# A spectral mixer in two halves: own tiles for x1 in the first images, half 1's inverse transforms and first loads ahead of the output blocks, and norms beside a transform

## The chip, the cores and the metric

The kernel runs on one core of one Trainium2 chip. The metric is the device time of one execution in microseconds, as the median of several runs. One core has five engines that work side by side, each through its own queue of instructions in order: TensorE (PE, with weight loads as PEld), VectorE (DVE), ScalarE (ACT), GpSimd (POOL) and SyncE (SP), which here only issues transfers. Transfers are also issued by ScalarE and GpSimd. A transfer that waits at the head of a queue holds up whatever stands behind it in that queue.

## The reference

The input x is an array of 256 x 256 pixels of 128 channels. Two layers are added to it one after the other. Layer 0 (a group norm and an attention with gate and biases) is not touched by the change. The result of layer 0 is x1, and layer 1 is `x1 + L1(gn(x1))`. It begins with a spectral attention over 256 tokens, images of 128 x 128 pixels, and ends with a mixer of four tokens at a time, to which the change belongs:

```python
attn = instance_norm(attn + tokens, attn_norm_w, attn_norm_b)
attn = attn.reshape(b * (C // TOKEN_CODIM), TOKEN_CODIM, H, W)      # groups of 4
h0 = instance_norm(attn, norm2_w, norm2_b)
h1 = fno_layer(h0, ..., norm=True, act=True)
h2 = fno_layer(h1, ..., norm=True)
out = instance_norm(h2, mon_w, mon_b) + attn
# fno_layer(x):
#   skip = einsum('bihw,oi->bohw', x, sw) + sb
#   xf   = instance_norm(spectral_conv(x))     # rfft2, 32 x 16 modes times weights, irfft2
#   y    = xf + skip;  gelu(y) if act
```

So each of the two spectral convolutions of the mixer takes an image to a few modes, mixes the modes within groups of four, and takes them back to an image. The norms in between need sums over the whole image, and so nothing can go from one stage to the next before all blocks of pixels are done.

## The kernel before, in words

Up to about 1,904 us the kernel computes layer 0, the attention of layer 1 and its modes. The mixer begins there. The 256 token images are taken in two halves, `a` = 0 and 1, of 128 images, one image to a partition. The 128 x 128 pixels of an image are split into 16 blocks of `NB` = 2,048 pixels (half a block is `HB` = 1,024). [...]`blocks`, also called `hb[b]`, holds 128 x 16 x 2,048 numbers. Half 1 waits in DRAM as `yd` in the meantime, and so does the residual of half 0 (x1 plus its scaled y) as `wd`. Half 1's images overwrite the blocks of half 0 as these are finished.

The mixer has these stages, each a Python generator that gives way at its `yield`s:

- `y_blocks(a)`: attn + tokens before its norm, one half block at a time, from x1 (`load_x1`, tag "xt") and inverse-transformed modes `gs`: matmuls L1324 and L1200 into `yps`, VectorE's scaling L1334 and statistics L1336. Half 0 goes to `blocks`, half 1 to DRAM (`yd`, L1338, issued by GpSimd).
- `first_modes(a)`: statistics of y (`bn_aggr`, L1418), two norm chains, the modes `F` of half a (loaded at L1412), then `mix_modes` (L1341): 16 products on VectorE (L1358), each with a matmul (L1367), squares (L1370), energy (L1376), the norm, and `Z` (L1399). Then the inverse transform over rows in four chunks (`synth_modes`), each written to DRAM as `Gd1` by copies L584 and transfers L589.
- `first_images(a)`: 16 blocks of `h1 = gelu(spectral part + skip)`: `gs2` loaded by L1217, matmuls L1211 and L1200 into `ups`, Gelu L1495 by ScalarE, four transposes L1504, copies to `hT`, the forward transform over columns `psA` L1527, its copy `yA` L1529 by ScalarE and the write to `Yd` L1530. For half 0 the residual is prepared beside it: `load_w` loads x1 (L1468, `xw`), `add_w` scales the block (L1475, ScalarE) into the second half of the same `xw` tile, adds (L1478, GpSimd) and writes `wd` (L1479). Its three buffers have the tag "xt". For half 1, `load` also brings y of the block from `yd` (L1461).
- `second_modes(a)`: loads `YT_0` to `YT_3` from `Yd` (L1546), transforms over rows (`f1ps`, L1563), copies to `F` (L1569), mixes as above with the second weights, four chunks to `Gd2`, and the last norm (`kap`, `c0`).
- `output_0` and `Output1`: per block the second inverse transform `h2ps`, ScalarE's scaling L1615, VectorE's add of the residual L1621 and the write L1622, issued by GpSimd. For half 1 the residual comes from `yd` and x1 at the time (L1659, L1663), and one VectorE instruction adds them (L1668). `Output1.ahead` does the first five of these during the second mixing.

The order of the work is written out by hand: inside `tc.manual_schedule` each engine keeps the order in which Python emits the instructions, and SyncE's queue is among them. `weave(main, side)` advances the second generator by the time the first says that it has used. The stages follow each other like this, with the times of the trace of before:

- y of half 0 (1,904 to 2,045 us), then first mixing of half 0 with 24 half blocks of y of half 1 (to 2,194), then the first images of half 0 (to 2,341).
- The last eight half blocks of y of half 1, woven with the forward transform of half 0 (to 2,402). Then both mixings at once, step by step in turn: second of half 0 (`m0`), first of half 1 (`m1`).
- Five output blocks of half 0, two steps after each chunk of `m1` (to about 2,533).
- The pools of this part are closed and `hp1` and `op0` opened, and first images of half 1 run beside the remaining output blocks of half 0 (to 2,705).
- Second mixing of half 1 (to 2,784), then its output (to the end).

The driver for the middle part, lines shortened by what does not matter here:

```python
m0 = second_modes(0, wp, tiles(wp), bq, [(xp, "xt", 3)])
weave((1.5 * t for t in iter(lambda: next(m0), None)), y1)
...
for _ in m0:
    next(m1)
...
for t in m1:
    next(o0)
    next(o0)
```

Of the kernel before, what the change touches and what calls it, by code (L numbers as in the profile page):

```python
# [18 lines left out]
P = 128  # L19
# [493 lines left out]
def layer1(tc, I, C, ident, x1d, upool, U, stats2, mv2, out):  # L513
# [9 lines left out]
    with ExitStack() as ctx:  # L523
# [712 lines left out]
        def run(stage):  # L1236
            for _ in stage:
                pass
# [213 lines left out]
        def first_images(a, wp, yp, psk, pst):  # L1452
# [12 lines left out]
            def load_w(b):  # L1465
                for s in range(2):
                    ys[b, s] = yp.tile([P, 2, HB], FP, tag="xt", name=f"xw_{b}_{s}", bufs=3)
                    nc.sync.dma_start(ys[b, s][:, 0], x1v[:, a, b * NB + s * HB : b * NB + (s + 1) * HB])  # L1468

            def add_w(b):  # L1470

                for s in range(2):
                    px = slice(b * NB + s * HB, b * NB + (s + 1) * HB)
                    t = ys.pop((b, s))
                    nc.scalar.activation(  # L1475
                        t[:, 1], hb[b][:, s * HB : (s + 1) * HB], AF.Identity, scale=h.col[:, 3:4]
                    )
                    nc.gpsimd.tensor_tensor(t[:, 1], t[:, 1], t[:, 0], ALU.add)  # L1478
                    nc.gpsimd.dma_start(wd[:, px], t[:, 1])  # L1479

            load(0)
# [54 lines left out]
        def second_modes(a, wp, mk, psum, gts, gbufs=1):  # L1536
# [6 lines left out]
            def load(c):  # L1543
                YT[c] = wp.tile([P, 2, 2, 512], FP, tag="gt", name=f"YT_{a}_{c}", bufs=gbufs)
                for hc in range(2):
                    nc.sync.dma_start(  # L1546
                        YT[c][:, hc],
                        h.Yd[P * hc : P * hc + P].rearrange("h (r f) t -> h r (f t)", r=2)[
                            :, :, 4 * c * P : 4 * (c + 1) * P
                        ],  # L1550
                    )
# [3 lines left out]
            if gbufs > 1:  # L1555
                load(1)
            for c in range(4):
# [12 lines left out]
                if c + gbufs < 4:  # L1570
                    load(c + gbufs)
                    yield 4.0
# [74 lines left out]
        class Output1:  # L1647
# [23 lines left out]
            def ahead(self):  # L1671
                self.more = self.wp
                for k in range(5):
                    self.load(k)
                    if k > 0:
                        self.add(k - 1)
                    yield 1.0
                self.add(4)
# [28 lines left out]
        with tc.manual_schedule(engines=COMPUTE | {ENG.SP}):  # L1707
# [8 lines left out]
            with yctx:  # L1716
# [7 lines left out]
                with tc.tile_pool(name="mp1", bufs=1) as wp:  # L1724
                    y1 = y_blocks(1, br, U1, 32)
                    next(y1)
                    m0 = second_modes(0, wp, tiles(wp), bq, [(xp, "xt", 3)])
                    weave((1.5 * t for t in iter(lambda: next(m0), None)), y1)
                    run(y1)
                    m1 = first_modes(  # L1730
                        1, wp, Tiles(F=(xp, "yt", 2), f=(xp, "yt", 2), m=(xp, "gs", 3)), br,
                        [(wp, "gt", 1), (xp, "xt", 3)],
                    )
                    for _ in m0:
                        next(m1)
# [3 lines left out]
                    for t in m1:  # L1739
                        next(o0)  # L1740
                        next(o0)
                    pools[3] = False
                    next(o0)
                    next(o0)
            with tc.tile_pool(name="hp1", bufs=2) as wp, tc.tile_pool(name="op0", bufs=4) as op:
                pools[:] = [op, wp, 4, True]
                due, begun = 0.0, False
                for done in first_images(1, wp, op, bq, br):
                    if not done:
                        due += 0.72  # L1750
                        begun = due > 0
# [6 lines left out]
            with tc.tile_pool(name="op1", bufs=2) as op:  # L1758
                o1 = Output1(op)
                with tc.tile_pool(name="mp3", bufs=1) as wp, tc.tile_pool(  # L1760
                    name="mpq3", bufs=8, space=PSUM
                ) as psq:
                    m1 = second_modes(1, wp, tiles(wp), Banks(psq, "q"), [(wp, "gt", 2)], gbufs=2)
                    run(iter(lambda: next(m1), None))
                    weave((0.4 for _ in m1), o1.ahead())
# [167 lines left out]
```

## Time and profile before

| | before |
|---|---|
| time, median of 3 runs | 2,918.85 us (2,915.04 to 2,921.63) |
| span of the profiled execution | 2,925.7 us, granted TensorE clock 0.944 |
| instructions | 70,150 |
| busy, share of the span: PE / PEld / DVE / ACT / POOL | 90% / 66% / 69% / 50% / 56% |
| bytes moved | 430.02 MB, 147 GB/s in the mean |

Shares of the whole span say little here, as two thirds of it belong to layer 0 and the attention. The table of windows, cut at the stages named above, gives the busy time in each:

| stage | from to, us | length | PE | DVE | ACT | POOL | DMA share | GB/s |
|---|---|---|---|---|---|---|---|---|
| y of half 0 | 1904 to 2045 | 141 | 139.2 | 87.3 | 0.0 | 0.0 | 0.87 | 278 |
| first mixing half 0, y of half 1 | 2045 to 2194 | 149 | 131.4 | 87.0 | 9.9 | 18.6 | 0.86 | 289 |
| first images half 0 | 2194 to 2341 | 147 | 130.1 | 82.7 | 73.7 | 105.6 | 0.87 | 290 |
| last y of half 1, transform of half 0 | 2341 to 2402 | 61 | 44.9 | 23.2 | 0.6 | 5.1 | 0.81 | 273 |
| both mixings | 2402 to 2471 | 69 | 54.1 | 43.2 | 9.4 | 6.0 | 0.30 | 90 |
| chunks of half 1, five output blocks | 2471 to 2533 | 62 | 28.2 | 16.7 | 19.4 | 11.5 | 0.78 | 262 |
| first images half 1, outputs half 0 | 2533 to 2705 | 172 | 150.5 | 94.2 | 81.1 | 23.3 | 0.85 | 292 |
| second mixing half 1 | 2705 to 2784 | 79 | 47.8 | 31.1 | 7.9 | 6.7 | 0.55 | 170 |
| output half 1 | 2784 to 2925 | 141 | 77.7 | 70.9 | 44.4 | 17.1 | 0.94 | 351 |

Read a row like this: busy times of engines are microseconds within the stage, so an engine whose number is near the length is full. "DMA share" is the mean busy share of the core's 16 transfer engines.

### The profile page before, as it was taken

The page shows a single profiled execution, that of the slowest core. Times are in us where ns is not written, and L with a number is a line of the kernel's source. Part 1 is how long each engine was busy: PE and PEld are TensorE (multiplying, and loading weights), DVE is VectorE, ACT ScalarE, POOL GpSimd, SP SyncE. Part 2 cuts the span into 40 slices and gives each one's busy share as a digit, 9 for nine tenths or more (in the row PEclk, how much of TensorE's full clock was granted, in tenths as well). Part 3 has the DMA queues.
Part 4 walks back from the last instruction along what each step waited for, and adds up shares of the span by engine and source line. Part 5 has one row for each costly group of instructions (what it writes and reads, how often), then busy time and mean ns, then how long its engine had stood idle before and what let it go on. Part 6 is the DMA issues. An engine that isn't in the chain of part 4 may idle for free. (4 is left out here: it accounts for less than half of the span.)

```text
span 2925.7 us, 70150 instructions
## 1 busy us (share of the span) xinstructions
PE 2638.9 (90%) x28524; PEld 1916.9 (66%) x28524; DVE 2007.8 (69%) x3239; ACT 1460.9 (50%) x2844; POOL 1647.0 (56%) x1282
## 2 busy tenths in 40 slices
PE   6799999999999999999999799999898868588654
PEld 6677777777777777777777567777574455344433
DVE  7787888888888888888788645656655545256345
ACT  0477777777777777777777413200005402244032
POOL 0399999999999999999999501100017701111011
PEclk9999999999999999999999899999999988699765
DMA  9422222222222222222222101388798964797599
GB/s 361 165 68 65 72 68 66 66 66 68 66 66 66 67 70 71 66 66 66 68 66 66 44 2 53 114 268 281 251 331 276 304 237 141 263 328 254 168 351 341
DMA packets 240955, 430.02 MB, mean 147 GB/s; under 512 B 26038, under 2 KB 169865, under 8 KB 232312
## 3 DMA queue, kind: packets, MB, share of 16 engines
q1 hardware_dynamic: 200184, 333.24, 34.3%
q0 software_dynamic: 23552, 83.90, 7.8%
q10 hardware_dynamic: 16896, 8.39, 1.0%
q8 instruction: 226, 3.70, 0.5%
q14 instruction: 97, 0.79, 0.1%
HBM read 290.17 MB, written 135.27 MB: 145 GB/s over the span
## 5 line engine op out<-in xcount | busy, mean ns | idle before, releaser
L299 POOL TENSOR_TENSOR e<-e,b1T 128x1024 f32<-128x1024 f32 x256 | 606.6, 2369 | 165.6 <-PE u L348 90.3
L303 POOL TENSOR_TENSOR es<-e 128x512 f32<-128x512 f32 x512 | 639.3, 1269 | 20.1
L281 ACT ACTIVATE sc<-sc,b2T 128x512 f32<-128x512 f32 x512 | 339.0, 662 | 365.5 <-PE sc L272 357.2
L323 DVE RECIPROCAL av<-av 128x256 f32<-128x256 f32 x256 | 452.3, 1767 | 27.2 <-DVE og L322 1.4
L281 ACT ACTIVATE e<-sc,b2T 128x512 f32<-128x512 f32 x512 | 348.0, 680 | 0.0
L294 DVE TENSOR_TENSOR e<-sc,b1T 128x1024 f32<-128x1024 f32 x256 | 311.0, 1215 | 0.0
L272 PE MATMUL sc<-qkT 32*128 32x256 f32 x4096 | 294.3, 401 | 1.3 <-DVE e L294 1.3
L311 PE MATMUL av<-e,v 128*32 128x256 f32 x4096 | 274.7, 385 | 0.5 <-POOL e L299 0.5
L1324 PE MATMUL yps<-xt,mpT 128*128 128x256 f32 x1024 | 244.5, 393 | 21.9 <-DVE yt L1334 11.1
L272 PEld LDWEIGHTS sc<-qkT 32*128 32x128 f32 x4096 | 185.6, 184 | 112.4 <-issue 97.8
L322 DVE SCALAR_TENSOR_TENSOR og<-gate,av 128x256 f32<-128x256 f32 x256 | 107.7, 421 | 190.5 <-PE av L316 190.5
L1324 PEld LDWEIGHTS yps<-xt,mpT 128*128 128x128 f32 x1024 | 194.1, 194 | 60.2 <-DVE yt L1334 14.2
L1338 POOL DMA_DIRECT2D yd<-yt x32 | 17.4, 545 | 358.0 <-DVE yt L1334 358.0
L327 POOL TENSOR_TENSOR x<-xt,bo 128x256 f32<-128x256 f32 x256 | 187.4, 732 | 0.0
L246 PE MATMUL qk<-xnT,wT_wq 128*128 128x256 f32 x512 | 179.5, 432 | 1.7 <-ACT xnT L238 1.7
L252 PEld LDWEIGHTS gv<-wT_wv,kvT 128*128 128x128 f32 x1024 | 155.0, 192 | 13.4
L316 PE MATMUL av<-es,ones 128*32 128x256 f32 x2048 | 157.5, 379 | 2.5 <-POOL es L303 2.5
L333 PE MATMUL wo<-wT_wo,og 128*128 128x128 f32 x1024 | 156.8, 276 | 2.7 <-DVE og L324 2.7
L1615 ACT ACTIVATE blocks<-h2ps,col 128x512 f32<-128x512 f32 x128 | 89.0, 777 | 140.4 <-PE h2ps L1200 140.4
L311 PEld LDWEIGHTS av<-e,v 128*32 128x32 f32 x4096 | 107.0, 109 | 76.1 <-POOL e L299 1.0
L348 PE MATMUL u<-adft,x 128*128 128x129 f32 x1024 | 156.4, 275 | 0.0
L252 PE MATMUL gv<-wT_wv,kvT 128*128 128x128 f32 x1024 | 156.0, 275 | 0.0
(524 smaller groups left out, 5199.4 us busy)
## 6 DMA issues: line engine op xcount, KB each, us to landing
xt<-x1d SPq DMA_DIRECT2D x128, 512.0 KB
xb<-in_x_dram SPq DMA_DIRECT2D x32, 1024.0 KB
xt<-in_x_dram SPq DMA_DIRECT2D x128, 256.0 KB
kt<-in_L_conv_kv_x_dram SPq DMA_DIRECT2D x128, 256.0 KB
x1d<-x SPq DMA_DIRECT2D x256, 128.0 KB
gs<-Gd SPq DMA_DIRECT2D x384, 64.0 KB
yd<-yt POOLq DMA_DIRECT2D x32, 512.0 KB, 5.2
xw<-x1d SPq DMA_DIRECT2D x32, 512.0 KB
```

Source lines behind the costliest of these rows:

```text
L246: nc.tensor.matmul(ps[:, 0:256], wT["wq"], xnT, start=True, stop=True)
L252: nc.tensor.matmul(ps[:, 256 + c * P : 256 + (c + 1) * P], kvT[:, c * P : (c + 1) * P], wT["wv"], start=True, stop=True,)
L272: nc.tensor.matmul(sc[h // 2][:, h % 2, c * 256 : (c + 1) * 256], qkT[p, 256 + c * P : 256 + (c + 1) * P], qkT[p, 0:256], start=True, stop ...
L281: nc.scalar.activation(r["e"][1][:, :, c, :] if hp else z, z, AF.Exp, bias=b2T[:, c, s : s + 1])
L294: nc.vector.tensor_tensor(r["e"][0].rearrange("p h c q -> p (h c q)"), r.pop("sc").rearrange("p h x -> p (h x)"), b1T[:, 0:2].rearrange("p ...
L299: nc.gpsimd.tensor_tensor(e1, e1, b1T[:, 2:4].rearrange("p h c q -> p (h c q)"), ALU.mult)
L303: nc.gpsimd.tensor_tensor(r["es"][hp], e[:, :, 0, :], e[:, :, 1, :], ALU.add)
L311: nc.tensor.matmul(ps[hd, 0:256], r["v"][:, c, hd], r["e"][h // 2][:, h % 2, c, :], start=(c == 0), stop=(c == 1),)
L316: nc.tensor.matmul(ps[32 * h : 32 * h + 32, 256:512], self.ones, r["es"][h // 2][:, h % 2, :], start=True, stop=True,)
L323: nc.vector.reciprocal(rd, rd)
L327: nc.gpsimd.tensor_tensor(r["x1"], r["x"], bc(self.bo, 1, 2), ALU.add)
L1324: nc.tensor.matmul(rows_of(ps[j]), mpT[:, sc, tt], by_turn(xt[:, sc])[:, j], start=(sc == 0), stop=False,)
```

## The change

The change reorders the mixer from the first images of half 0 on, and gives some tiles buffers of their own. The arithmetic and the bytes moved stay the same. It has five parts:

- A, own tiles for x1 in `first_images`. x1's two halves are loaded to tags that other stages had left unused in this one ("yt", two buffers, and a new "xw" with one), and the scaled block gets a whole-block tile `w0` in the three "xt" buffers. Both of ScalarE's scalings go before both of GpSimd's adds. This is meant to free ScalarE from waiting for a write of `wd`.
- B, the norms beside the transform. `second_modes` is told which buffers its four `YT` tiles take. Half 0 now has four of them, and loads 1 after the first transform and 2 and 3 after the second. The last y blocks end before the third transform, and the norm chains of half 1 (`first_modes(1)`) are emitted between the second and the third transform.
- C, half 1's inverse transforms ahead of the output. `m1` runs to its end before output blocks are begun. y and `gs2` of half 1's first block are loaded into tiles of the mixing's pool (`y2`, `g2`), and so they need not wait for the next pools. Two output blocks instead of five come before the change of pools.
- D, as a consequence, more output blocks (14 rather than 11) are run between the images of half 1: the rate is `due += 0.9` instead of 0.72.
- E, in the second mixing of half 1, `Output1.ahead` issues its first two loads at once and does its five adds only after the 16 products of `mix_modes`. The `YT` loads 2 and 3 follow the first and second transform as before.

```diff
-        def first_images(a, wp, yp, psk, pst):
+        def first_images(a, wp, yp, psk, pst, first=None):
...
             def load_w(b):
                 for s in range(2):
-                    ys[b, s] = yp.tile([P, 2, HB], FP, tag="xt", name=f"xw_{b}_{s}", bufs=3)
-                    nc.sync.dma_start(ys[b, s][:, 0], x1v[:, a, b * NB + s * HB : b * NB + (s + 1) * HB])
+                    t = (yp, "yt", 2) if s == 0 else (wp, "xw", 1)
+                    ys[b, s] = t[0].tile([P, HB], FP, tag=t[1], name=f"xw_{b}_{s}", bufs=t[2])
+                    nc.sync.dma_start(ys[b, s], x1v[:, a, b * NB + s * HB : b * NB + (s + 1) * HB])
 
             def add_w(b):
 
+                t = yp.tile([P, NB], FP, tag="xt", name=f"w0_{b}", bufs=3)
                 for s in range(2):
-                    px = slice(b * NB + s * HB, b * NB + (s + 1) * HB)
-                    t = ys.pop((b, s))
-                    nc.scalar.activation(
-                        t[:, 1], hb[b][:, s * HB : (s + 1) * HB], AF.Identity, scale=h.col[:, 3:4]
-                    )
-                    nc.gpsimd.tensor_tensor(t[:, 1], t[:, 1], t[:, 0], ALU.add)
-                    nc.gpsimd.dma_start(wd[:, px], t[:, 1])
-
-            load(0)
+                    px = slice(s * HB, (s + 1) * HB)
+                    nc.scalar.activation(t[:, px], hb[b][:, px], AF.Identity, scale=h.col[:, 3:4])
+                for s in range(2):
+                    px = slice(s * HB, (s + 1) * HB)
+                    nc.gpsimd.tensor_tensor(t[:, px], t[:, px], ys.pop((b, s)), ALU.add)
+                    nc.gpsimd.dma_start(wd[:, b * NB + s * HB : b * NB + (s + 1) * HB], t[:, px])
+
+            if first is None:
+                load(0)
+            else:
+                ys[0], gss[0] = first
...
-        def second_modes(a, wp, mk, psum, gts, gbufs=1):
+        def second_modes(a, wp, mk, psum, gts, yts):
...
             def load(c):
-                YT[c] = wp.tile([P, 2, 2, 512], FP, tag="gt", name=f"YT_{a}_{c}", bufs=gbufs)
+                yp, tag, bufs = yts[c]
+                YT[c] = yp.tile([P, 2, 2, 512], FP, tag=tag, name=f"YT_{a}_{c}", bufs=bufs)
...
-            if gbufs > 1:
+            if a:
                 load(1)
...
-                if c + gbufs < 4:
-                    load(c + gbufs)
+                for k in ((2,), (3,), (), ())[c] if a else ((1,), (2, 3), (), ())[c]:
+                    load(k)
+                if c < 3:
                     yield 4.0
...
             def ahead(self):
                 self.more = self.wp
+                self.load(0)
+                self.load(1)
+                yield 1.0
                 for k in range(5):
-                    self.load(k)
-                    if k > 0:
-                        self.add(k - 1)
+                    self.add(k)
+                    if k < 3:
+                        self.load(k + 2)
                     yield 1.0
-                self.add(4)
...
-                    m0 = second_modes(0, wp, tiles(wp), bq, [(xp, "xt", 3)])
-                    weave((1.5 * t for t in iter(lambda: next(m0), None)), y1)
+                    m0 = second_modes(
+                        0, wp, tiles(wp), bq, [(xp, "xt", 3)], [(wp, "gt", 1)] * 3 + [(xp, "xt", 3)]
+                    )
+                    weave((2.4 * next(m0) for _ in range(3)), y1)
                     run(y1)
                     m1 = first_modes(
-                        1, wp, Tiles(F=(xp, "yt", 2), f=(xp, "yt", 2), m=(xp, "gs", 3)), br,
-                        [(wp, "gt", 1), (xp, "xt", 3)],
-                    )
+                        1, wp, Tiles(F=(xp, "yt", 2), f=(xp, "yt", 2), m=(xp, "gs", 3)), br, [(xp, "xt", 3)]
+                    )
+                    for _ in range(3):
+                        next(m1)
+                    run(iter(lambda: next(m0), None))
                     for _ in m0:
                         next(m1)
                     pools = [xp, xp, 3, True]
                     o0 = output_0(pools, bq)
                     next(o0)
-                    for t in m1:
+                    y2 = wp.tile([P, NB], FP, tag="gt", name="y2_0", bufs=1)
+                    nc.sync.dma_start(y2, ydv[:, 1, 0:NB])
+                    run(m1)
+                    g2 = wp.tile([P, 4, P], FP, tag="m", name="gs2_1_0", bufs=2)
+                    next(o0)
+                    load_modes(g2, halves[1].Gd1, 0)
+                    pools[3] = False
+                    for _ in range(3):
                         next(o0)
-                        next(o0)
-                    pools[3] = False
-                    next(o0)
-                    next(o0)
-            with tc.tile_pool(name="hp1", bufs=2) as wp, tc.tile_pool(name="op0", bufs=4) as op:
+            with tc.tile_pool(name="op0", bufs=4) as op, tc.tile_pool(name="hp1", bufs=2) as wp:
                 pools[:] = [op, wp, 4, True]
                 due, begun = 0.0, False
-                for done in first_images(1, wp, op, bq, br):
+                for done in first_images(1, wp, op, bq, br, (y2, g2)):
                     if not done:
-                        due += 0.72
+                        due += 0.9
                         begun = due > 0
...
-                    m1 = second_modes(1, wp, tiles(wp), Banks(psq, "q"), [(wp, "gt", 2)], gbufs=2)
+                    m1 = second_modes(1, wp, tiles(wp), Banks(psq, "q"), [(wp, "gt", 2)], [(wp, "gt", 2)] * 4)
                     run(iter(lambda: next(m1), None))
-                    weave((0.4 for _ in m1), o1.ahead())
+                    ahead = o1.ahead()
+                    next(ahead)
+                    for k, _ in enumerate(m1):
+                        if k >= 16:
+                            next(ahead, None)
+                    run(ahead)
```

## The prediction, made before the changed kernel was run

> **What bounds the kernel now.** I read the page first: its row of 40 slices shows that from about slice 27 on (1,904 us) no engine is solid, and the DMA row goes down to 1 and 3. The change touches only what begins at 2,184 us, so I cut that part by stage with the table of windows, and then read waits and timeline where a stage has gaps. The window columns are the busy time of PE, PEld, DVE, ACT and POOL, the granted clock, the DMA share and GB/s.
>
> ```profile
> 2218.00:2270.00 52.00, 47.48 (x728) 24.13 (x720) 30.32 (x49) 27.65 (x42) 38.73 (x31) 1.00 0.89 299
> 2345.00:2362.00 17.00, 9.91 (x45) 7.33 (x44) 4.02 (x9) 0.00 (x0) 1.10 (x2) 0.70 0.91 316
> 2400.00:2440.00 40.00, 30.72 (x75) 14.39 (x76) 28.85 (x65) 3.08 (x6) 0.53 (x1) 0.87 0.07 25
> 2505.00:2520.00 15.00, 6.43 (x64) 3.52 (x56) 2.36 (x2) 3.37 (x6) 1.64 (x3) 0.72 0.68 217
> 2520.00:2533.00 13.00, 0.23 (x16) 0.26 (x32) 2.36 (x2) 2.27 (x3) 1.06 (x2) 0.50 0.59 201
> 2610.00:2660.00 50.00, 43.09 (x722) 25.16 (x720) 25.46 (x37) 21.01 (x37) 6.49 (x11) 0.90 0.96 333
> 2732.00:2760.00 28.00, 20.48 (x50) 8.65 (x50) 17.70 (x31) 2.94 (x5) 0.00 (x0) 0.87 0.32 114
> 2850.00:2900.00 50.00, 31.72 (x352) 20.50 (x352) 27.75 (x23) 14.20 (x21) 6.07 (x12) 0.57 1.03 386
> ```
>
> Where blocks stream (rows 1, 2, 6, 8) the transfers are at 0.9 and more, and there the rest hangs on bytes. Between them lie stretches where the DMA idles: the mode mixing, the change-over before half 1's images, the second mixing. A microsecond saved there is a microsecond of the end, since what follows is bound by bytes that have to move anyway.
>
> In half 0's images (from 2,194 us) the timeline and the waits show one loop:
>
> ```profile
> 2264.97 1.15 ACT L1475 ACTIVATE xw<-blocks,col 128x1024 f32<-128x1024 f32 x1 [2.59 <-DMA wd<-xw]
> 2266.03 0.57 ACT L1529 COPY yA<-psA 128x512 f32<-128x512 f32 x1
> 2266.65 0.42 PEld L1504 LDWEIGHTS htps<-ident,blocks 128*128 128x128 f32 x4 [1.38 <-ACT yA L1529]
> ...
> SPq L1468 <- DMA wd<-xw: 80.5, 25, 9.6
> ```
>
> ScalarE's scaling of the next block waits until an old xw buffer has been written out; the copy yA stands behind it in ScalarE's queue, and TensorE's transposes wait for the PSUM bank that yA frees. The starts of ups in that timeline run from 2,218.60 to 2,323.29 us in 12 blocks, 8.72 us each; a block without a stall takes 8.00 (2,270.11 to 2,278.11).
>
> At the change-over to half 1:
>
> ```profile
> 2521.01 1.28 ACT L1495 ACT_TABLE_LOAD   x1
> 2527.10 0.34 SPq L1461 DMA_DIRECT2D y<-yd  x1
> 2532.77 2.02 PE L1211 MATMUL ups<-y,bl 32*32 32x512 f32 x32 [14.20 <-DMA gs<-Gd]
> 2545.34 3.89 PE L1211 MATMUL ups<-y,bl 32*32 32x512 f32 x32 [0.46 <-ACT blocks L1615]
> ```
>
> The first load of half 1 is issued at 2,527, when the new pools' memory is free, which takes the output writes of all blocks before. In the second mixing VectorE's adds for the output stand between the products that TensorE waits for:
>
> ```profile
> 2736.90 1.28 DVE L1668 SCALAR_TENSOR_TENSOR x<-y,col,x 128x1024 f32<-128x1024 f32 x1
> 2737.03 0.43 PEld L1367 LDWEIGHTS z1acc<-z1m,ident 128*128 128x128 f32 x2 [0.65 <-DVE z1m L1358]
> 2759.72 1.29 DVE L1399 TENSOR_TENSOR z1Z<-z1acc,z1rsb 128x512 f32<-128x512 f32 x2 [1.18 <-ACT z1rsb L1396]
> ```
>
> **What the Trainium skill says.** "Perfetto Trace Analysis", section Optimization Strategy: the same gap again and again on the engine that should be full can mean too few buffers for the next tile, and stages with different limits may gain from interleaving. The trace agrees with both: 25 waits of the queue on wd in half 0, and DMA shares of 0.07 and 0.96 in neighbouring stages. "DMA: Bandwidth & Descriptors", section Issuing engines are not separate DMA queues: the transfers of SP, ScalarE and GpSimd share 16 engines. So moving a load ahead adds no bandwidth where the share is 0.96; it fills only idle stretches. The same page, section Anatomy of one DMA, puts most of a transfer's fixed 2 us into the confirmation of the last byte; here under load it is far more, 4.9 us median from issue to landing for wd and 8.0 for the output.
>
> **The change part by part.**
>
> A, half 0's images. The x1 halves get tiles freed by GpSimd's add, and the scaled block a tile of its own in three buffers, so ScalarE waits for a write three blocks old: no stall. Instructions and bytes stay. New waits: xw half 1 has one buffer, so its load waits for the add (2.36 us), and the next block's four gs loads are queued behind it in SP. Add 2.4 plus load 4.5 to 5 (a load issued at about 2,265.0, its add starts at 2,269.89) is 7.3 us, under 8. But bytes then bind: x1 1.05, wd 1.05, gs 0.26, Yd 0.26 is 2.62 MB a block, 8.1 us at 323 GB/s (the mean of 2,552 to 2,660 us). I take 8.35 for 8.72 to 8.9: 13 blocks give 7 us. At the start gs of block 1 is now behind xw, whose slot waits for a yd write issued at 2,191.3 (landing 5.2): 1 to 2 us lost. Net -6.
>
> B, the last eight y blocks with the transform. With GpSimd no longer late, the last yA needn't wait for a Yd write (it waited 8.6 us, TensorE 2.3), so Yd lands and YT_0 is issued some 4 us sooner after the last psA (2,337.1). YT_2 and YT_3, 2.1 MB or 6.5 us at 323 GB/s, go behind the last x1 load, so the y blocks, short of data (row 2), end about 55 us after that psA, not 64.8 (2,401.9). Behind them, bn_aggr and the two norm chains (2,403.1 to 2,411.9, 8.6 us on VectorE) now run alone while YT_2 and YT_3 land, where before they stood between products. -10 for the end of the y blocks; products of half 0 then start 9.5 us after it rather than at once, while half 1's start 14 after it rather than 16.1. By the lockstep of 1.72 us a pair (VectorE and TensorE rows at 2,421 to 2,433) half 0's Z comes at +45 rather than +41.5.
>
> C, the eight inverse transforms in one go, two output blocks instead of five, then half 1. Eight chunks write 1.05 MB each: at 300 GB/s or by three xt buffers (copy 1.3, issue 1.5, landing 5.2) about 3.3 us a chunk, so the last is written at about +79. y of block 0 is loaded before, its gs lands at +84, and block 0 of the images runs at +84, where it stood at +131 (2,532.8). Then a new wait: y of block 1 needs the new pool, hence the output write of block 1: DVE done +86.5, landing 8 later, so +94; gs of output block 2 is behind it in SP, at +103, and ups of block 1 at +105.5 against +143.4 (2,545.3). That is 38 us sooner with three outputs fewer done.
>
> D, the rest of the images. An image costs y 1.05, gs 0.26, Yd 0.26 = 1.57 MB; an output w 1.05, gs 0.26, out 1.05 = 2.36. Before, 16 images and 10 outputs were 48.8 MB in 159.5 us (2,545.3 to 2,704.8), 306 GB/s. Now 13 outputs: 55.8 MB. At 306 it is 182 us; block by block, 13 x 12.2 us (3.93 MB at 323, TensorE needs 9.4) plus three short ones of 6.5, 6.5 and 5 is 177. I take 180: +20. With C, -17 (38 less 20 is 18, less 1 for pool order: YT_0's first half could be issued at 2,694 and now waits for the whole pool).
>
> E, the second mixing. Five adds of 1.28 leave the products: 6.4 us. They go under ScalarE's squares and TensorE's energy sums (2,752.7 to 2,756.6, room for two), the norm's broadcast (1.2) and the first chunk. Loads of blocks 2 to 4 now follow the adds; landing 3.5 us, just in time. -5, and the output stage (386 GB/s, unchanged) moves up by that.
>
> Sum: -6 - 10 - 17 - 5 = -38. I take 3 off for chained estimates: 2,918.85 - 35 = 2,884 us.
>
> **Rivals.** R1, less comes through (bytes): C's gap lasts until +112 and D runs at 295 GB/s (189 us), so that C and D give 2 instead of 17; A and B half, 8; E 5. That is -15, 2,904 us. For: every later stage is at 0.9. Against: 0.96 was held at 2,610 to 2,660. R2, a new wait takes over: the single xw buffer with a landing of 8 us makes a loop of 10.4 us, 15 x 1.7 = 25 us more in A, and D runs at 285 GB/s (196 us, 36 more, C and D together -2 + 1 = -1); with B -10 and E -5 it is +9, 2,928, slower. For: output writes do take 8 us. Against: xw loads landed in 5 with more bytes queued. R3, streaming improves: A at 8.0 (-11), D at 345 GB/s (162 us, 18 better), B and E as above: 2,862. For: 386 GB/s at the end, with large rows. Against: Yd and gs go in short rows. R4, gains and losses cancel, within 6 us.
>
> **How the numbers follow.** The forecast 0.60, R1 0.20, R3 0.09, R2 0.08, R4 0.03. The range reaches from near R3 to past R1: 2,858 to 2,913; outside are R2, R4 and the far end of R3, some 0.17. Faster by over 0.2% (5.8 us): 0.60 + 0.20 + 0.09 = 0.89; same 0.03; slower 0.08.
>
> **What would show it.** In the after profile: ups of half 0 every 8.1 to 8.5 us and no wait of ScalarE on wd; ups of half 1's block 0 some 84 us after the last y block's statistics, with the longest gap of TensorE just behind it, waiting for gs; about 12.3 us per image with an output at a DMA share over 0.9; z1Z about 5 us sooner after the F copies. Blocks at 9 us or more in A, or an image with output at 14, make it wrong.

## The result, and the profile after

The changed kernel takes 2,897.23 us in the median of 4 runs (2,893.59 to 2,898.90), against 2,919.83 us (2,915.04 to 2,921.63) for the kernel before in the same call. The ratio is 0.9923, with a 95% interval of 0.9906 to 0.9941. Run once more beside other kernels it gave 0.9913 (0.9897 to 0.9930). So the change is worth some 22 to 25 us. The forecast was 35 us, 2,884, with a range that holds 2,897.

The profiled execution of after has a span of 2,896.1 us at a granted clock of 0.948. Both profiled executions of before (the second is experiment e1) have 2,925.7 and 2,926.8 us at 0.944 and 0.945; the times of these two executions, 2,927.72 and 2,928.78 us, are 9 to 10 us over the median of that kernel. The two traces therefore differ by 29.6 us, more than the kernels do. Executions of one kernel lie some 20 us apart (2,908.40 to 2,929.82 us for before in one call), and among the fourteen of e1 the longest, 2,928.78 us, had a granted clock of 0.945 and the shortest, 2,911.64 us, one of 0.952.

The table of windows of the kernel after, cut where the work stands that the prediction showed of before. Columns: window, length, busy time of PE, PEld, DVE, ACT and POOL, granted clock, DMA share, GB/s.

```profile
2218.00:2270.00 52.00, 51.44 (x792) 26.60 (x784) 30.51 (x51) 28.89 (x43) 41.35 (x32) 1.00 0.93 316
2341.00:2357.00 16.00, 11.67 (x63) 8.67 (x61) 3.87 (x9) 0.00 (x0) 1.10 (x2) 0.79 0.99 332
2390.00:2430.00 40.00, 32.77 (x87) 15.28 (x87) 28.03 (x67) 3.17 (x8) 0.00 (x0) 0.91 0.03 8
2450.00:2480.00 30.00, 19.56 (x507) 14.18 (x510) 7.32 (x23) 6.84 (x14) 7.46 (x11) 0.67 0.96 284
2486.00:2500.00 14.00, 9.54 (x119) 3.57 (x111) 2.36 (x2) 6.13 (x9) 1.06 (x2) 0.69 0.50 182
2566.00:2660.00 94.00, 83.18 (x1572) 46.11 (x1584) 55.50 (x77) 48.53 (x84) 15.42 (x25) 0.98 0.97 345
2706.00:2732.00 26.00, 19.05 (x70) 8.31 (x70) 18.72 (x34) 2.94 (x5) 0.00 (x0) 0.89 0.31 105
2800.00:2870.00 70.00, 43.08 (x496) 27.19 (x480) 37.83 (x32) 20.42 (x31) 8.16 (x16) 0.55 1.03 385
```

In half 0's images TensorE is now full, 51.4 of 52 us (47.5 before), with the transfers at 0.93. Row 3 is the mixing, where the transfers idle as before. Row 4 holds the chunks of the two transforms, with writes from two queues and the loads of output block 0 and of y beside them: a stretch in which the transfers are full while TensorE works 19.6 of 30 us (before had 0.84 in the same window and 0.90 from 2,471 to 2,501 us). Row 5 is the new hole behind block 0 of half 1. Row 6, half 1's images with the output, moves more than before (345 GB/s at 0.97, against 333 at 0.96). The last row is unchanged.

Half 0's images in the timeline of after (start, length, engine, line and operation, and in brackets the idle time ahead and what ended it):

```profile
2262.75 2.20 ACT L1476 ACTIVATE w<-blocks,col 128x1024 f32<-128x1024 f32 x2
...
2263.45 1.17 SPq L1469 DMA_DIRECT2D xw<-x1d  x1
...
2263.59 2.35 POOL L1479 TENSOR_TENSOR w<-w,xw 128x1024 f32<-128x1024 f32 x1 [2.10 <-DMA xw<-x1d]
...
2266.08 1.16 PE L1211 MATMUL ups<-blocks,bl 32*32 32x512 f32 x32
```

and the waits of SyncE's queue and of one copy of ScalarE between 2,200 and 2,330 us (who waited for whom: us in total, times, longest):

```profile
SPq L1469 <- POOL w L1479: 43.0, 16, 3.3
SPq L1469 <- DMA xw<-x1d: 17.2, 12, 2.8
ACT yA L1533 <- DMA Yd<-yA: 37.1, 12, 5.7
```

ScalarE's two scalings run back to back, with no wait for a landing of wd. SyncE waits for the single second xw buffer 16 times, up to 3.3 us, as was expected of it. In place of the wait on wd ScalarE has a new one: its copy yA waits 12 times, 37.1 us in all, for a write of Yd to land (no such wait in before between 2,194 and 2,338 us). What sets the pace of a block is not shown: the transfers are at 0.93, TensorE is marked busy nearly throughout, and single blocks take from 7.4 to 9.5 us.

The change-over to half 1 in the timeline of after:

```profile
2487.77 3.73 PE L1211 MATMUL ups<-y,bl 32*32 32x512 f32 x32 [0.46 <-ACT blocks L1621]
...
2492.42 0.53 POOL L1628 DMA_DIRECT2D out_dram<-w  x1 [0.59 <-DVE w L1627]
...
2495.95 0.34 SPq L1461 DMA_DIRECT2D y<-yd  x1
2496.46 3.31 SPq L1217 DMA_DIRECT2D gs<-Gd  x4
2499.81 0.42 SPq L1637 DMA_DIRECT2D w<-wd  x1
2500.27 4.03 SPq L1217 DMA_DIRECT2D gs<-Gd  x4
...
2508.09 2.73 PE L1200 MATMUL h2ps<-k_bsyn,gs 32*128 32x128 f32 x32 [10.09 <-DMA gs<-Gd]
```

Block 0 begins 45 us sooner than before (2,532.8). Then y of block 1 is issued only when output block 1 has been written, the modes of output block 2 come behind it, and TensorE waits 10.09 us: the wait that the prediction named.

The second mixing, VectorE in the timeline of after:

```profile
2720.89 0.69 DVE L1358 TENSOR_TENSOR z1m<-F,mixwr 128x512 f32<-128x512 f32 x1 [0.17 <-PE z1acc L1367]
2721.50 2.47 DVE L1674 SCALAR_TENSOR_TENSOR x<-y,col,x 128x1024 f32<-128x1024 f32 x2
2725.21 0.16 DVE L35 TENSOR_SCALAR rq_ve<-z1ens 128x1 f32<-128x1 f32 x1 [1.24 <-PE z1ens L1376]
...
2729.14 1.28 DVE L1399 TENSOR_TENSOR z1Z<-z1acc,z1rsb 128x512 f32<-128x512 f32 x2
```

The adds stand behind the products, two of them inside ScalarE's squares and TensorE's energy sums: VectorE still waits 1.24 us after them.

### The profile page after: what moved, and what is told of

It is laid out like the page before. It is cut to its first block, busy times and chain, and to the rows that moved or that the text cites. A ratio compares the mean times of both kernels' runs of the same rounds, so it can differ in the third digit from the quotient of the medians.

```text
span 2896.1 us, 70186 instructions
## 1 busy us (share of the span) xinstructions
PE 2640.4 (91%) x28524; PEld 1920.0 (66%) x28524; DVE 2007.2 (69%) x3239; ACT 1463.0 (51%) x2844; POOL 1647.4 (57%) x1282
## 5 line engine op out<-in xcount | busy, mean ns | idle before, releaser
L1324 PEld LDWEIGHTS yps<-xt,mpT 128*128 128x128 f32 x1024 | 194.5, 195 | 59.1 <-DVE yt L1334 16.3
```

Of the source, the lines that this page charges most:

```text
L1324: nc.tensor.matmul(rows_of(ps[j]), mpT[:, sc, tt], by_turn(xt[:, sc])[:, j], start=(sc == 0), stop=False,)
```

## The experiments

Times are medians. "Before" in each call was 2,918.8 (e1 to e4), 2,918.8 (e5 to e8) and 2,916.9 us (e9 to e12). Single executions of one kernel lie up to 10 us apart on either side, so a difference of 3 us between two medians of six is not told from none. Therefore each part is also followed in its stage of the trace. The work ahead of the first ups of half 0 is the same in all runs and ends between 2,187.9 and 2,194.6 us in their traces; the last row of the second table leaves this scatter out.

| run | us | ratio to before, 95% interval |
|---|---|---|
| e1 before again | 2918.84 | 0.9999 (0.9986 to 1.0013) |
| e2 A undone | 2897.72 | 0.9928 (0.9905 to 0.9951) |
| e3 E undone | 2896.51 | 0.9915 (0.9893 to 0.9937) |
| e4 early y and modes, rate undone | 2900.82 | 0.9931 (0.9906 to 0.9955) |
| e5 B undone | 2899.09 | 0.9926 (0.9900 to 0.9952) |
| e6 y loaded before the mixings | 2889.00 | 0.9896 (0.9867 to 0.9924) |
| e7 as e6, w behind the chunks | 2892.66 | 0.9911 (0.9886 to 0.9937) |
| e8 three outputs ahead | 2893.80 | 0.9913 (0.9885 to 0.9941) |
| e9 A and E alone | 2904.80 | 0.9962 (0.9948 to 0.9976) |
| e10 C and D undone | 2904.08 | 0.9951 (0.9936 to 0.9967) |
| e11 as e6, one output ahead | 2877.44 | 0.9863 (0.9841 to 0.9885) |
| e12 after again | 2894.05 | 0.9913 (0.9897 to 0.9930) |

Stages in us, from the timelines (differences of the first starts of the instructions named; "stat" is the end of the last statistics of y, "psA" the end of the last forward transform of a half, and the last F copy is also taken at its end):

| stage | before | e1 | after | e12 | e5 | e10 | e6 | e11 |
|---|---|---|---|---|---|---|---|---|
| first ups of half 0 to psA | 142.7 | 149.1 | 137.5 | 136.8 | 138.2 | 140.1 | 140.1 | 140.2 |
| psA to stat | 64.9 | 65.7 | 55.1 | 57.5 | 60.1 | 57.0 | 54.2 | 52.3 |
| stat to half 0's row transform | 41.5 | 41.5 | 45.5 | 45.5 | 41.6 | 46.6 | 45.5 | 45.5 |
| to half 1's first chunk | 24.3 | 25.1 | 14.6 | 14.3 | 23.0 | 23.0 | 12.9 | 14.7 |
| to ups of block 0 | 65.0 | 65.9 | 41.0 | 41.5 | 33.8 | 65.2 | 37.7 | 27.1 |
| to ups of block 1 | 12.6 | 11.6 | 23.5 | 22.9 | 23.6 | 11.8 | 21.4 | 21.2 |
| to psA of half 1 | 159.4 | 156.5 | 167.5 | 163.4 | 170.1 | 157.4 | 161.9 | 168.2 |
| to the last F copy | 26.9 | 26.8 | 27.8 | 26.3 | 25.5 | 24.7 | 26.8 | 25.2 |
| to the row transform of half 1 | 30.0 | 27.6 | 24.4 | 24.2 | 24.4 | 24.0 | 25.9 | 24.3 |
| to the end | 164.1 | 162.8 | 165.0 | 165.0 | 164.6 | 163.4 | 163.4 | 166.4 |
| first ups of half 0 to the end | 731.4 | 732.6 | 702.1 | 697.5 | 704.9 | 713.1 | 689.9 | 685.0 |

**e1, the kernel before again.** No edit.

> The kernel before, profiled once more. The two profiles differ by 29.6 us (2925.7 to 2896.1), the medians by 22.6. Theory P (the trace of before is a sample on the long side, and some 7 us of the differences between the two traces are not the change's): a span of 2916 to 2920, shorter than the first profile in the streaming stages behind 2,471 us. Rival Q (profiling itself adds that time to the kernel before): a span of 2924 to 2927 again, with ups of half 1's block 1 near 2,545 and its last psA near 2,704.

The span was 2,926.8 us, so Q's number came, though at other places: half 0's images took 6 us longer than in the first trace, the second mixing 2.4 us less. Two of two profiled executions of before lay 9 to 10 us above the median; with executions that reach from 2,908 to 2,930 us that may be chance, and whether profiling adds to it stays open. Two traces of one kernel differ by up to 6 us in one stage, which is the grain of every stage comparison here.

**e2, A undone.** The old tiles and order in `load_w` and `add_w`:

```diff
-                    t = (yp, "yt", 2) if s == 0 else (wp, "xw", 1)
-                    ys[b, s] = t[0].tile([P, HB], FP, tag=t[1], ...)
+                    ys[b, s] = yp.tile([P, 2, HB], FP, tag="xt", ..., bufs=3)
```

> After with part A undone: xw and its scaled block share three xt tiles again, scaling and add go by halves. Theory P (part A saves what its stage shows, since later stages start later by it): first images of half 0 take 129 us from first to last ups instead of 123.3, and the time is 2897 + 6 = 2903. Rival Q (the wait for bytes takes the saving back in the y blocks behind it): 2897 to 2899.

The stage from the first ups to psA was 146.5 us against 137.5, so A does what it was to do. The median rose by 0.5 us only, which is Q's number; but the intervals leave room for P's 6 us. From the first ups of half 0 to the end its trace takes 706.0 us, 3.9 and 8.5 more than the two traces of after, which is P's; and e9 below shows A and E to be worth 12 together. This run alone does not decide.

**e3, E undone.** `ahead()` and its `weave` as before.

> After with part E undone: loads and adds for the output woven into the products of the second mixing again. Theory P (VectorE's five adds stand in TensorE's way): from the last F copy to the first row transform of Z 30.4 us instead of 24.9, and 2897 + 5 = 2902. Rival Q (the output stage is bound by its transfers and takes it back): 2897 to 2899.

From the last F copy to the row transform 27.4 us against 24.4, with the median unchanged. E saves some 3 us in its stage by this pair, 5.6 by the first traces. From the first ups to the end the trace takes 706.5 us, 4.4 and 9.0 more than those of after. Its share of the time isn't resolved by this run.

**e4, the early loads and the rate undone.** The edit was meant to undo C and D whole, but keeps half 1's three steps of lead, so that only the last chunk is left to alternate with outputs: two output blocks still come before half 1's images. The edit changes results too: with 0.72 outputs per image, images overtake the output, so from output block 8 on the output is computed from blocks that half 1 has already overwritten. The work is the same.

```diff
-                    y2 = wp.tile(...); nc.sync.dma_start(y2, ydv[:, 1, 0:NB])
-                    run(m1)
-                    g2 = wp.tile(...); load_modes(g2, halves[1].Gd1, 0)
+                    for t in m1: next(o0); next(o0)
...
-                        due += 0.9
+                        due += 0.72
```

> After with parts C and D undone: five output blocks between the chunks of half 1, y and gs of block 0 loaded from the new pools, 0.72 outputs per image; A, B and E stay. Theory P (the prediction's step, 17 us): 2914. Theory Q (the two traces: half 1's last psA gained 25.9 us, of which the end of the y blocks had 15.3, so 10.6): 2908. Rival R (B's gain was only to be had with C, or C and D cancel): 2897 to 2902.

So its time does not answer the question it was made for (e10 comes closer). But its trace shows something of value. Without the early y and modes, block 0 of half 1 began 24.6 us after output block 0 (19.3 in after), and block 1 only 11.4 us later (23.5): counted from output block 0, block 1 came 6.8 us sooner than in after. So the early load of y, as the change placed it, may not have paid; but another wait, shown under e7, is missing in this trace as well, and e4 does not separate the two.

**e5, B undone.** One YT buffer, all four transforms woven with the y blocks, half 1's norms in step with half 0's mixing.

```diff
-                    weave((2.4 * next(m0) for _ in range(3)), y1)
+                    weave((1.5 * t for t in iter(lambda: next(m0), None)), y1)
...
-                    for _ in range(3): next(m1)
-                    run(iter(lambda: next(m0), None))
```

> After with part B undone: one buffer for half 0's YT tiles, all four transforms woven with the y blocks, half 1's norm chains only when the mixing of half 0 has begun. Theory P (the prediction's step: only the end of the y blocks and half 0's Z count, 6 us): 2903. Theory Q (what counts is when half 1's transform begins, since everything behind it hangs on its chunks; in the two traces it came 21 us earlier, of which A had 5.6): 2907 to 2912, and first chunk of half 1 some 131 us after the last psA of half 0 instead of 115.

Half 1's first chunk came 124.7 us after psA against 115.2 (60.1 + 41.6 + 23.0, and 55.1 + 45.5 + 14.6): 9.5 us of B's saving, as Q said. But ups of block 0 came 33.8 us after it against 41.0, so that 2.4 us of it remained there: B's lead is spent in the stretch of the chunks. A wait of ScalarE of 6.9 us in after, shown under e7, is 0.4 us in e5 and has the size of what is lost. The time, 2 to 5 us over after, is nearer P's 6 us, which its interval holds, than Q's.

**e6, y of block 0 loaded before the mixings.** The one load moves in SyncE's queue from 2,467.4 us to 2,388.1, just ahead of where row 3 above shows a DMA share of 0.03.

```diff
+                    y2 = wp.tile([P, NB], FP, tag="gt", name="y2_0", bufs=1)
+                    nc.sync.dma_start(y2, ydv[:, 1, 0:NB])
                     for _ in m0:
                         next(m1)
...
-                    y2 = wp.tile(...); nc.sync.dma_start(y2, ydv[:, 1, 0:NB])
                     run(m1)
```

> After with one edit: the load of y of half 1's block 0 is issued before the two mixings instead of between the chunks. Theory P (the write of half 1's last chunk waits for ScalarE's write before it to land, whose 11.5 us are long because 2 MB of w and y go beside it; the wait itself stays): the last write is issued 2 to 3 us sooner, ups of block 0 2 to 3 us sooner, 2894. Rival Q (bytes alone count: 1 MB out of a full stretch): 4 us or more, 2892. Rival R (block 1's wait for the new pools sets the pace and takes it all back): 2896 to 2897.

2,889.0 us, and ups of block 1 5.4 us sooner after the first chunk (59.1 against 64.5). The traces of e2, e3 and e12, whose code in this stretch is that of after, have 61.6, 63.7 and 64.4, so that 2.5 to 5.4 us are the edit's. The interval of the time reaches 0.9924 and overlaps that of after, so that R is refuted by the stage and not by the time. Nor did the wait stay, as P had it:

```profile
2467.21 1.07 ACT L584 COPY g11gt<-g11gp 128x512 f32<-128x512 f32 x2 [2.12 <-PE g11gp L576]
2469.28 3.01 ACTq L589 DMA_DIRECT2D Gd<-g11gt  x2
2472.34 2.78 ACT L1621 ACTIVATE blocks<-h2ps,col 128x512 f32<-128x512 f32 x4 [4.05 <-PE h2ps L1200]
```

The copies end at 2,468.3 and the first of the last two writes is issued at 2,469.3, 1.0 us later, where after waits 6.9 us (the lines under e7). So e6 takes 1 MB out of the stretch and most of that wait with it, and does not tell P's cause from Q's.

**e7, also w and modes of output block 0 behind the last chunk.** In the trace of after ScalarE's writes of the last chunk are held up, and its queue with them:

```profile
2468.54 1.07 ACT L584 COPY g11gt<-g11gp 128x512 f32<-128x512 f32 x2 [2.37 <-PE g11gp L576]
2476.48 1.39 ACTq L589 DMA_DIRECT2D Gd<-g11gt  x2
2477.92 2.79 ACT L1621 ACTIVATE blocks<-h2ps,col 128x512 f32<-128x512 f32 x4 [8.31 <-DMA Gd<-g11gt]
```

The copies end at 2,469.6; the writes are issued from 2,476.5 on, by the profile when a write of the chunk before has landed. The wait stands in all five traces that have this order of the transfers: 6.9 us in after, 7.8 in e12, 7.7 in e2, 7.0 in e3, 7.1 in e8. Output block 0 is then scaled 31.2 to 31.5 us after the first chunk, and 21.7 to 27.0 in e4, e5, e6 and e11, which lack the wait (0.4 to 1.0 us). e7 adds to e6 another order of the transfers:

```diff
-                    next(o0)                 # w and modes of output block 0
                     run(m1)
+                    next(o0)
```

> After with y of block 0 loaded before the mixings, and the loads of output block 0 (w and its modes) issued behind the last chunk of half 1 instead of before it. ScalarE's last two writes of a chunk then wait for no landing of the writes before them. Theory P (that wait, 6.9 us in the trace of after, stands in front of ScalarE's scaling of output block 0 and so of all that follows): last write of half 1's chunks 6 us sooner, ups of block 0 at 94 us after the last y statistics instead of 101, ups of block 1 at 118 instead of 125, 2891. Rival R (the loads that now come later, and bytes behind them, take it back): 2895 to 2898.

The wait was gone, in the timeline of e7:

```profile
2468.28 1.07 ACT L584 COPY g11gt<-g11gp 128x512 f32<-128x512 f32 x2 [2.12 <-PE g11gp L576]
2469.72 1.17 ACTq L589 DMA_DIRECT2D Gd<-g11gt  x2
2477.10 2.79 ACT L1621 ACTIVATE blocks<-h2ps,col 128x512 f32<-128x512 f32 x4 [7.74 <-PE h2ps L1200]
```

and nothing came of it beyond e6: output block 0 was scaled at 2,477.1, now late because its own modes were; ups of block 0 at 97 us after stat (96 in e6); the median within the interval of e6. But e6 had only 1.0 us of the wait left, so that e7 does not price it. P's mechanism is real: what it costs in after is between nothing and its whole 6.9 us, and no run takes it away alone.

**e8, three output blocks ahead instead of two**, and 0.87 per image.

> After with three output blocks instead of two before half 1's images, and 0.87 outputs per image instead of 0.9 behind. Theory P (the hole behind block 0 is a wait for the new pools, which stays as long; one output more is done before it, one fewer behind): ups of block 0 and of block 1 some 8 us later, images with outputs 8 to 10 us shorter, time equal within 3 us: 2895 to 2899. Rival Q (fewer outputs ahead was what part C lives from): 2902 or more.

Counted from stat, ups of block 0 came 5.3 us later than in after and of block 1 2.4 us later, less than P's 8; the images took 164.4 us, within those of after (167.5 and 163.4) and not 8 to 10 us less; the time was equal to after's within the intervals, as P had it.

**e9, A and E alone**, on the kernel before.

> The kernel before with parts A and E alone. Theory P (parts add up as their stages show: A 5.6, E 5.5): 2919 - 11 = 2908, and B, C and D together give the other 11 or 12. Theory Q (undone one at a time, A and E cost 1 to 5 us each, so their savings are partly taken back behind them): 2910 to 2915, and B, C and D are worth 14 or more together.

12.1 us, by the interval 7 to 15: P's 11 lie in the middle, and of Q's 4 to 9 only the upper end is left. So A and E together are worth what their stages show; neither was run alone on the kernel before, and how the sum divides is open.

**e10, C and D undone as a whole.** As e4, but with half 1's mixing three steps behind, so that its four chunks alternate with output blocks 0 to 3 and the output keeps ahead of the images.

```diff
                     for k, _ in enumerate(m0):
-                        next(m1)
+                        if k >= 3:
+                            next(m1)
```

> After with C and D undone as a whole, in the order of before: half 1's mixing three steps behind, its four chunks each followed by one output block, y and modes of block 0 from the new pools, 0.72 outputs per image; A, B and E stay. Theory P (the prediction's step): 17 us more than after, 2914. Theory Q (the two traces, 10.6): 2908. From the last y statistics to half 1's last psA some 300 us instead of 292. Rival R (C alone lost what D gained): 2897 to 2901.

2,904.08 against 2,894.05 us for after in the same call: 10 us, Q's number. It takes B's lead of three steps with it: half 1's first chunk comes 126.5 us after psA, for 115.2 in after. So the 10 us are those of C, D and that lead together. It stands at the same time as e9 (2,904.80), which lacks B altogether: what e10 keeps of B is worth nothing that can be measured.

**e11, e6 with one output block ahead**, one per image behind.

```diff
-                    next(o0)
                     load_modes(g2, halves[1].Gd1, 0)
                     pools[3] = False
-                    for _ in range(3):
-                        next(o0)
+                    next(o0)
+                    next(o0)
...
-                        due += 0.9
+                        due += 1.0
```

> The kernel with the early load of y of block 0, and with one output block instead of two before half 1's images, one output per image behind. Theory P (bytes in the chunks' stretch are what counts, and w and modes of output block 1, 1.3 MB or 4 to 5 us, leave it; images with an output cost 10.9 us against 10.7 without, so one more behind costs little): ups of block 0 at 88 to 92 us after the last y statistics instead of 96, time 2885. Rival Q (the wait for the new pools then stands ahead of output block 1 and takes it back): ups of block 1 no earlier than 117 after the statistics, time 2889 to 2893.

2,877.44 us, 0.9863 of before, the fastest of all. TensorE around the change-over in the timeline of e11:

```profile
2472.59 3.76 PE L1211 MATMUL ups<-y,bl 32*32 32x512 f32 x32 [0.66 <-ACT blocks L1621]
...
2483.40 3.21 PE L1211 MATMUL h2ps<-blocks,blk 32*32 32x512 f32 x32 [1.60 <-ACT blocks L1499]
2490.87 2.42 PE L1200 MATMUL h2ps<-k_bsyn,gs 32*128 32x128 f32 x32 [4.26 <-DMA gs<-Gd]
2493.78 3.07 PE L1211 MATMUL ups<-y,bl 32*32 32x512 f32 x28 [0.49 <-ACT blocks L1621]
```

and two rows of its table of windows, the chunks and the hole behind them:

```profile
2450.00:2480.00 30.00, 21.54 (x494) 14.06 (x496) 9.48 (x24) 7.28 (x13) 8.00 (x12) 0.71 0.91 271
2480.00:2494.00 14.00, 7.64 (x94) 4.63 (x98) 0.00 (x0) 4.40 (x7) 0.00 (x0) 0.62 0.89 310
```

ups of block 0 at 87 us after stat (2,472.6 less 2,385.3), block 1 at 108. The wait for the modes of the next output block fell to 4.26 us: y of block 1 is issued at 2,481.7, 3.5 us behind the last write of output block 0, and no longer waits for output block 1. The transfers of the hole run at 0.89, where after had 0.50 behind block 0. Rival Q is refuted, and P's 2,885 passed by 8 us. e11 takes away at once the bytes of output block 1, its place ahead of block 0 in TensorE's queue and the wait for its write; it does not tell these apart.

**e12, after again.** No edit.

> The changed kernel once more, beside the other runs. Both theories: 2894 to 2899; the stages of its trace within 2 us of the first, so that 292 us from the last y statistics to half 1's last psA and 24.5 from the last F copy to the first row transform of Z stand as what the change does. If they move by more, differences of single parts below that can't be told.

2,894.05 us. Stages within 2.4 us of the first trace, but for half 1's images (4.1 less). That is more than the 2 us allowed above, so that in the long stages a difference of some 4 us between two single traces tells nothing. The stretch from the first chunk to ups of block 1 agrees better, 64.5 and 64.4 us.

## Why the prediction came out as it did

The direction and the range held; 35 us were forecast, 22.6 measured, and in the same call as e12 22.8.

**A (-6).** Right in size. The blocks run at 8.21 us (12 from 2,218.73 to 2,317.29; 8.44 in e12) for a forecast of 8.35, with no wait on wd; the stage is 5.2 us shorter, and A and E alone give 12.1 us (e9) for the 11 of the two terms. That bytes bind there, as forecast, is not shown, and the wait of yA on Yd was not foreseen.

**B (-10).** The stage went as worked out: the y blocks end 55.1 us after psA (55 forecast; 57.5 in e12), half 0's Z begins 45.5 us later (45). With A in place B has only half of it: with A and without B they end 60.1 and 60.3 us after psA (e5, e9), and not at 65. What failed is the step that carries these 10 us to the end. Undoing B costs 2 to 5 us (e5). Half 1's transform begins 9.5 us sooner through B, and 7 of them are gone when block 0 begins: ScalarE's last writes wait 6.9 us with their data ready in after, and 0.4 us in e5; no run takes this wait away alone.

**C (38 us sooner at block 1).** The mis-sized term, with the most in it. The forecast had the last chunk written at 79 us after stat, ups of block 0 at 84 and of block 1 at 105.5. In after the last write was issued at 91, ups of block 0 came at 101.1 and of block 1 at 124.6, 18.8 us sooner than before and not 38. The term "about 3.3 us a chunk" took 8.4 MB of writes at 300 GB/s and nothing beside them. Three things stand in that stretch which it left out:

- w and modes of output block 0 and y of block 0 (1.05 + 0.26 + 1.05 = 2.36 MB) go through it, at 284 GB/s an estimated 8.3 us, and the modes and w of output block 1 behind them.
- ScalarE's last writes wait 6.9 us for an earlier write to land, and the scaling of output block 0 stands behind them.
- Output blocks 0 and 1 stand ahead of ups of block 0 in TensorE's queue.

That C lost its time here is shown by e6 and e11. With y's load gone, and most of the wait with it, block 1 comes 2.5 to 5.4 us sooner after the first chunk; with output block 1 gone as well, another 10.8 (59.1 to 48.3). With both, block 0 begins at 87, close to the 84 of the forecast. How the loss divides among the three is open, since e6 changes the first two together and e11 the first and the third.

From what the Trainium skill says in "DMA: Bandwidth & Descriptors", section Issuing engines are not separate DMA queues, that all these transfers run on the same 16 engines, the prediction had itself drawn that a load moved ahead gains only where the transfers idle. It did not ask that of the change's own early load, which lands in a stretch at 0.96.

**D (+20).** Too dear by more than half. Block 1 to psA took 167.5 us against 159.4, 8 us for three outputs more, and 163.4 against 156.5 in the second pair. The forecast priced an image with an output at 12.2 us by 323 GB/s and one without at 5 to 6.5. Measured from one start of ups to the next: 10.9 us with an output in after at 345 GB/s; and in before, 10.5 us with and 10.7 without (10.7 and 9.4 in e1). So images without output were not cheap: the window of one of them in before, 2,566.8 to 2,578.4, has a share of 1.00 at 354 GB/s, with transfers of the outputs around it. That is the fullest case: another, 2,640.6 to 2,649.8, takes 9.2 us at 0.80, so that bytes alone do not explain their price. So C gave 19 us less than forecast and D took 12 less, and the two errors largely cancel: in the traces C and D together give 10.7 us, and e10 has 10 with B's lead in it, for a forecast of 17. That the number came as near as it did is in part luck.

**E (-5).** Right by the traces, 30.0 to 24.4 us, though the second trace of before has 27.6, so 3 to 5.6.

In times: A and E gave 12 us for 11, and B, C and D together 11 (e9 against e12) for 27, of which 3 had been taken off.

Of the rivals, R1 (bytes bind, 2,904) had C's longer gap, to 112 us after stat where 124.6 were measured, and the time lies between it and the forecast; but its D at 295 GB/s did not come. D went as R3 had it, at 345 GB/s (162 us there, 167.5 and 163.4 measured). R2's loop of the single xw buffer did not come: the queue waits up to 3.3 us, and the blocks keep to 8.2; the new wait in this stage is that of yA on Yd.

## What to carry to other kernels

Before a load is moved ahead, look at the DMA share of the stretch that it lands in, and at what its place in the order does to other transfers: 1 MB issued 79 us earlier, from a stretch at 0.96 to the edge of one at 0.03, brought the next stage 2.5 to 5.4 us forward, in part perhaps because a wait of another queue went with it. Savings of stages in a row need not add up: of 9.5 us that B gained ahead of the chunks 2.4 were left behind them. Work out all megabytes of the stretch in which they meet, and not the writes alone, and look there for waits with data ready. And where output work stands between two stages, ask how little of it can go ahead: with one block instead of two, and the early load, the kernel takes 0.9863 of before (0.9841 to 0.9885), clear of the 0.9913 of after in the same call. Against e6 (0.9896) the intervals still touch; in the traces, counted from the first chunk, 10.8 us are gained at block 1 and 4.5 are left at half 1's psA, as the images take one output more.

## What the runs showed of the hardware

A DMA share near 1 is no one rate. In the chunks' stretch of after (2,450 to 2,480 us) 0.96 went with 284 GB/s, in the output stage 1.03 with 385 GB/s. Small packets explain a part of this only. ScalarE's writes of the chunks, 2.72 MB in packets of 512 bytes, took 34.2% of the 16 engines' time in that stretch, and GpSimd's, 3.15 MB of the same kind of data in packets of 4,096 bytes, took 34.1%: worked out, 60 and 52 us of one engine for a megabyte. In the output stage GpSimd's packets of 4,096 bytes took 41 (8.33 MB, 30.2% of 70 us). Why they are slower among the chunks is open.

A transfer that ScalarE issues can wait for the landing of one that it issued before, with data ready for 6.9 us, and what is behind it in ScalarE's queue waits with it. The semaphore numbers in the traces fit: the transfers of SyncE and ScalarE report on eight semaphores in turn, and in after the last two writes have the same two as the two writes before them, issued some 12 us earlier. In e7, with no wait, they share theirs with transfers issued 17 us or more before. So the number of unrelated loads in SyncE's queue can decide whether a write waits.
